# A third product of halves in block form, and the additions of bv moved behind the block sums

## The chip, the cores and the metric

The kernel runs on one core of one Trainium2 chip. A core has TensorE (matrix products, into PSUM), VectorE, ScalarE, GpSimd, and SyncE with the DMA queues. In profile lines they are PE (PEld for weight loads), DVE, ACT, POOL and SP. Each engine works through its own list of instructions in order, and semaphores hold an instruction back until the data it needs, or the buffer it overwrites, is free. The metric is the device time of one execution in microseconds, and less is better.

## The reference

The input `x` has 128 batches of a 128 x 512 matrix (128 nodes, 512 features). All values are float32. Layer 0 normalises each row, takes the positive part, multiplies by the adjacency matrix and adds the largest value per node to `x`. Layer 1 is attention with 8 heads of 64 over the 128 nodes.

```python
# layer 0
h = jnp.maximum(_layernorm(x, axis=-1), 0.0)
A = jnp.einsum('od,bdn->bon', adj, h); C = A + b[None, :, None]
pre = A[:, :, None, :] + (C - A)[:, :, :, None]
x = x + jnp.max(jax.nn.relu(pre), axis=-1)
# layer 1
h = jnp.maximum(_layernorm(x, axis=-1), 0.0)
q = (h @ Wq + bq); k = (h @ Wk + bk); v = (h @ Wv + bv)   # 8 heads of 64
scores = einsum('bihd,bjhd->bhij', q, k) / 8, masked where adj == 0
x = x + einsum('bhij,bjhd->bihd', softmax(scores), v)
```

In layer 0, `A` cancels in `pre`, and what is left per node is the positive part of the largest value of `C`. It adds the same number to all features of a node, so the second normalisation gives the same `h` as the first. That is why the kernel normalises only once.

## The kernel before

The 128 batches go through in 32 groups of four. `x` sits in SBUF in pairs of batches. Each group goes through these steps:

- `norm` and `norm_end`: statistics on VectorE (`bn_stats`, `bn_aggr`, `+eps`), `rstd` and `nmr` on GpSimd, then `h = relu(x*rstd + nmr)` on ScalarE. `norm_end` also calls `add_bv`, a GpSimd addition of bv to `x` for the output.
- `blocks` and `move`: h is transposed in 32 x 32 blocks by VectorE, and 16 DMAs per pair of batches put the blocks into `hT`.
- `adjacency`: one TensorE product, then a maximum on VectorE.
- `Products`: the three projections q, k, v of a group.
- `scores`: q against k, with `exp` on ScalarE; `mask` multiplies by the pattern of the adjacency, on GpSimd.
- `apply`: weights against v, with reciprocal and scaling on VectorE; `residual` adds `x` and writes out.

**The projections.** A projection is a product of a 512 x 512 weight with the group's `hT`. It is cut into quarters, and the four quarters of the result come from seven products of halves, in Winograd's form of Strassen's method, in place of eight. The sums of weight quarters (`s1` to `s4`, `weight_sum`) are made once. The sums of h quarters (`t1` to `t4`, `h_sum` at L340, tile `hs`) are made once per group on VectorE. The products are:

- `p1` = a11·b11
- `p6` = s2·t2
- `p2` = a12·b21
- `p7` = s3·t3
- `p5` = s1·t1
- `p4` = a22·t4
- `p3` = s4·b22

Each is four matmuls of 128 x 128 x 256, written by `mm` (L413 to L425), so eight block products of 128 x 128 x 128. `p4` and `p3` are cut once more by the same method, into seven block products each (`p43a` at L492, `p43b` at L511, matmuls in `block_mm` at L487). For that GpSimd makes block sums of t4 and b22 (`h_blocks` at L347) and, once, block sums of the weights (`weight_blocks` at L361). Parts that several output blocks share go to a scratch bank of PSUM, bank 6, and VectorE adds them on with `more` (L489 to L490). The first and the last group's v uses the plain `p4` and `p3`.

**Order.** The order is written out by hand. Iteration `g` runs `apply(g - 1)`, `scores(g)`, then v of group g and q and k of group g + 1. The 18 entries of `part` (6 for v, 6 for q, 6 for k, numbered 0 to 17 and called steps here) are run in turn, and after each the entries of `todo` for that step. Until the change the sums `t1` to `t4` stand at steps 0, 1, 2, 2 and the block sums at 5 and 6 (for g > 0). `next_norms` places the norms of the batches of group g + 2.

**Buffers.** PSUM has eight banks. v and k use banks 0, 1, 2 for `self.a`, `self.b`, `self.c`, and q uses 3, 4, 5. `hs` is in a pool with two buffers, and `h2` in one with one.

Of the kernel before, what the change touches and what calls it, by code (L numbers as in the profile page):

```python
# [45 lines left out]
F32 = mybir.dt.float32  # L46
# [6 lines left out]
P = 128  # L53
G = 4
H, HD = 8, 64
# [112 lines left out]
def tile_adj_preln_d2(  # L168
# [14 lines left out]
    B, D, N = x.shape  # L183
# [4 lines left out]
    const = ctx.enter_context(tc.tile_pool(name="const", bufs=1))  # L188
# [1 line left out]
    W = {n: const.tile([P, NC, N], F32, name=f"w{n}_sb") for n in "qkv"}  # L190
    WS = {n: const.tile([P, 4, 2, N // 2], F32, name=f"s{n}_sb") for n in "qkv"}

    WB = {n: const.tile([P, 2, 4, P], F32, name=f"ss{n}_sb") for n in "qkv"}
    b0_sb = const.tile([P, 1], F32, name="b0_sb")
    bq_sb = const.tile([P, NC], F32, name="bq_sb")
    bk_sb = const.tile([P, NC], F32, name="bk_sb")
# [10 lines left out]
    def fast(ctx):  # L207
        xpool = ctx.enter_context(tc.tile_pool(name="xpool", bufs=7))
        proj = ctx.enter_context(tc.tile_pool(name="proj", bufs=2))
        one = ctx.enter_context(tc.tile_pool(name="one", bufs=1))  # L210
# [6 lines left out]
        X, HN, TB, HT, HB, H2, QT, KT, C, AMAX, WA, RSTD, NMR, PR = ({} for _ in range(14))  # L217

        def bank(k):

            return ps.tile([P, 512], F32, name=f"bk{k}")
# [63 lines left out]
            nmr = NMR[m] = stat.tile([P, 1], F32, name="nmr")  # L285
            nc.gpsimd.tensor_scalar(nmr, mv[:, 0:1], rstd, -1.0, op0=ALU.mult, op1=ALU.mult)  # L286

        def norm_end(m):
            nc.scalar.activation(HN[m], x_of(m), AF.Relu, scale=RSTD[m], bias=NMR[m])  # L289
            if m >= G:  # L290
                add_bv(m)

        def add_bv(m):
# [52 lines left out]

        def h_blocks(g, k):  # L347

            if k == 0:
                H2[g] = one.tile([P, 2, 4, D], F32, name="h2")  # L350
            b = HB[g]["b22 t4".split()[k]].rearrange("p t c d -> p c t d")
            t = H2[g][:, 1 - k]

            for o, x, y in (
                (t[:, 0:2], b[:, :, 1], b[:, 0]),
                (t[:, 2], b[:, 1, 1], t[:, 0]),
                (t[:, 3], b[:, 1, 0], t[:, 2]),
            ):
                nc.gpsimd.tensor_tensor(o, x, y, op=ALU.subtract)

        def weight_blocks(eng, n):  # L361

            for k in range(2):
                a = WA[n]["a22 s4".split()[k]].rearrange("p c (o f) -> p o c f", o=2)
                s = WB[n][:, k]
                for o, x, op, y in (
                    (s[:, 0], a[:, 1, 0], ALU.add, a[:, 1, 1]),
                    (s[:, 2], s[:, 0], ALU.subtract, a[:, 0, 0]),
                    (s[:, 1], a[:, 0, 0], ALU.subtract, a[:, 1, 0]),
                    (s[:, 3], a[:, 0, 1], ALU.subtract, s[:, 2]),  # L370
                ):
                    eng.tensor_tensor(o, x, y, op=op)
# [19 lines left out]
        class Products:  # L392
# [78 lines left out]
            def block_views(self):  # L471

                self.wa = [
                    WA[self.n][k].rearrange("p c (o f) -> p o c f", o=2) for k in ("a22", "s4")
                ]
                self.hb = [
                    HB[self.g][k].rearrange("p t c d -> p c t d") for k in ("t4", "b22")
                ]
                self.scr = bank(6).rearrange("p (m k d) -> p m k d", m=2, k=2)
                o_t = "(o d) -> p {} o t d" if self.n == "v" else "(t d) -> p {} o t d"  # L480
                r = "t" if self.n == "v" else "o"
                self.ub = self.u.rearrange(f"p k {r} " + o_t.format("k"), d=D)
                self.bk = lambda x: x.rearrange(f"p {r} " + o_t.format(""), d=D)

            def block_mm(self, out, w, h, start=False):
                lhs, rhs = (h, w) if self.n == "v" else (w, h)
                nc.tensor.matmul(out, lhs, rhs, start=start, stop=True, skip_group_check=True)  # L487

            def more(self, to, what):  # L489
                nc.vector.tensor_tensor(to, to, what, op=ALU.add)  # L490

            def p43a(self):  # L492

                self.block_views()
                s, t = WB[self.n], H2[self.g]
                for k in range(2):
                    self.block_mm(
                        self.scr[:, 0, k], self.wa[k][:, 0, 0], self.hb[k][:, 0, 0], start=k == 0
                    )
                for k in range(2):  # L500
                    self.block_mm(self.scr[:, 1, k], s[:, k, 0], t[:, k, 0])
# [8 lines left out]

            def p43b(self):  # L511

                s, t, u, scr = WB[self.n], H2[self.g], self.ub, self.scr
                bc = [self.bk(self.b), self.bk(self.c)]
                for k in range(2):
                    self.block_mm(scr[:, 0, k], s[:, k, 2], t[:, k, 2])
                self.more(u[:, :, 0, 1], scr[:, 0])
                for k in range(2):
                    a, b = self.wa[k], self.hb[k]
                    self.block_mm(bc[k][:, 0, 0], a[:, 0, 1], b[:, 1, 0])  # L520
                    self.block_mm(bc[k][:, 0, 1], s[:, k, 3], b[:, 1, 1])
                    self.block_mm(bc[k][:, 1, 0], a[:, 1, 1], t[:, k, 3])
                for k in range(2):
# [120 lines left out]
        def next_norms(m):  # L644

            return {
                0: [(norm_end, m), (norm_end, m + 1)],
                4: [(blocks, m)], 6: [(blocks, m + 1), (move, m + 1)], 7: [(adjacency, m)],
                8: [(norm, m + 2), (norm_end, m + 2)],
                12: [(norm, m + 3), (norm_end, m + 3), (adjacency, m + 1)],  # L650
                13: [(blocks, m + 2)],
                14: [(blocks, m + 3), (move, m + 3), (adjacency, m + 2)],
            }

        with tc.manual_schedule():
# [31 lines left out]
            k = Products(0, "k")  # L687
# [12 lines left out]
            for g in range(NG):  # L700
                b = g * G
# [108 lines left out]
```

## Time and profile before

| | us |
|---|---|
| median of 10 runs | 1539.22 |
| lowest, highest | 1538.95, 1540.11 |
| profiled execution | 1538.79 |
| its span, first to last instruction | 1537.0 |

The groups of instructions that matter to the steps below, from the page (count, busy time, mean of one):

| line, engine, tiles, shape | count | busy us | mean ns |
|---|---|---|---|
| L490 DVE, u += scratch bank, 128x256 | 552 | 205.5 | 413 |
| L345 DVE, sums of h, 128x512 | 128 | 152.8 | 1194 |
| L469 DVE, sum of `p7`, 128x512 | 95 | 65.3 | 687 |
| L279 DVE, statistics, 128x512 | 128 | 87.5 | 683 |
| L302 DVE, transposition of h, 128x512 | 124 | 83.7 | 693 |
| L295 POOL, bv, 128x512 | 128 | 186.2 | 1465 |
| L582 POOL, mask, 128x512 | 240 | 297.3 | 1271 |
| L359 POOL, block sums of h, 128x256 | 62 | 45.2 | 728 |
| L359 POOL, block sums of h, 128x128 | 124 | 57.8 | 466 |

The page counts busy time per engine over the whole span. A mean can mix two durations: L345 has a median of about 695 ns and a longest of 1766 ns. The trace models the ends of matmuls, so rows of TensorE that follow each other overlap by 0.1 to 0.2 us, and the starts give their spacing. One group takes about 47.4 us: v starts at 803.76 us in the group used below, q at 817.28, k at 829.90.

### The profile page before, as it was taken

What the parts mean: (1) busy time and instruction counts of PE and PEld (TensorE: products, weight loads), DVE (VectorE), ACT (ScalarE), POOL (GpSimd) and SP (SyncE); (2) the same over time, 40 slices, a digit from 0 to 9 for tenths busy, and PEclk for the clock granted to TensorE, in tenths of its full rate; (3) what the DMA queues carried; (4) which work ended last, traced back from release to release, by engine and by line L of the source; (5) the groups of instructions that cost most, each with busy time, mean ns of one, the idle gap of its engine ahead of it and who ended that gap; (6) DMA issues with size and microseconds to landing.
All of it is one profiled execution on the core that took longest, in us unless ns stands there. A gap on an engine that the chain in (4) does not pass through costs nothing. (4 is left out here: it accounts for less than half of the span.)

```text
span 1537.0 us, 33066 instructions
## 1 busy us (share of the span) xinstructions
PE 1506.2 (98%) x12909; PEld 1321.0 (86%) x12909; DVE 1079.0 (70%) x2187; ACT 506.9 (33%) x970; POOL 869.5 (57%) x968
## 2 busy tenths in 40 slices
PE   8999999999999999999999999999999999999997
PEld 6888888888888888888888888888888888888887
DVE  6677677776767767677767777676676767776676
ACT  4333324333233332333332333324333233333332
POOL 5676556556575565655655655656556465565620
PEclk9999999999999999999999999999999999999999
DMA  5222222223222232222322222322223222232211
GB/s 169 60 62 77 63 60 72 65 74 84 42 73 66 72 82 43 76 74 63 79 59 63 74 63 75 74 51 72 65 72 84 42 74 68 70 80 54 52 34 57
DMA packets 307806, 105.32 MB, mean 69 GB/s; under 512 B 273152, under 2 KB 273280, under 8 KB 307648
## 3 DMA queue, kind: packets, MB, share of 16 engines
q1 hardware_dynamic: 307328, 102.84, 26.1%
q8 instruction: 104, 1.70, 0.5%
q14 instruction: 54, 0.44, 0.1%
q0 software_dynamic: 176, 0.27, 0.1%
q10 hardware_dynamic: 144, 0.07, 0.0%
HBM read 37.03 MB, written 33.55 MB: 46 GB/s over the span
## 5 line engine op out<-in xcount | busy, mean ns | idle before, releaser
L630 POOL TENSOR_TENSOR o<-xp,o 128x512 f32<-128x512 f32 x122 | 151.0, 1268 | 312.6 <-DVE o L618 269.3
L582 POOL TENSOR_TENSOR w<-w,live 128x512 f32<-128x512 f32 x240 | 297.3, 1271 | 0.0
L490 DVE TENSOR_TENSOR u<-u,bk 128x256 f32<-128x256 f32 x552 | 205.5, 413 | 120.4 <-PE bk L487 113.3
L578 ACT ACTIVATE w<-bk 128x512 f32<-128x512 f32 x256 | 128.8, 628 | 345.9 <-PE bk L570 345.9
L295 POOL TENSOR_TENSOR xp<-xp,bv_sb 128x512 f32<-128x512 f32 x128 | 186.2, 1465 | 61.3 <-ACT hn L289 60.4
L421 PEld LDWEIGHTS bk<-hs,sk_sb 128*128 128x128 f32 x768 | 143.6, 190 | 44.7 <-issue 29.4
L421 PE MATMUL bk<-hs,sk_sb 128*128 128x256 f32 x768 | 181.3, 379 | 0.0
L421 PE MATMUL bk<-sv_sb,hs 128*128 128x256 f32 x768 | 181.2, 379 | 0.0
L421 PE MATMUL bk<-hs,sq_sb 128*128 128x256 f32 x744 | 175.8, 379 | 0.0
L421 PEld LDWEIGHTS bk<-sv_sb,hs 128*128 128x128 f32 x768 | 143.6, 190 | 31.1 <-issue 14.3
L328 DVE TENSOR_REDUCE amax<-bk 128x1 f32<-128x512 f32 x128 | 88.1, 689 | 105.6 <-PE bk L327 102.7
L421 PEld LDWEIGHTS bk<-hs,sq_sb 128*128 128x128 f32 x744 | 138.9, 190 | 17.6
L284 POOL TENSOR_TENSOR rstd<-ve,mhalf 128x1 f32<-128x1 f32 x128 | 83.5, 653 | 94.2 <-DVE ve L282 93.9
L289 ACT ACTIVATE hn<-xp,nmr,rstd 128x512 f32<-128x512 f32 x124 | 100.7, 813 | 105.0 <-POOL nmr L286 105.0
L469 DVE TENSOR_TENSOR u<-bk,u 128x512 f32<-128x512 f32 x95 | 65.3, 687 | 91.8 <-PE bk L421 89.7
L327 PE MATMUL bk<-hn,adjT 128*128 128x512 f32 x248 | 126.6, 592 | 0.0
L600 PE MATMUL bk<-v,w 128*64 128x65 f32 x4096 | 126.5, 222 | 0.0
L600 PEld LDWEIGHTS bk<-v,w 128*64 128x64 f32 x4096 | 122.1, 137 | 4.1 <-issue 0.3
L421 PE MATMUL bk<-wv_sb,hT 128*128 128x256 f32 x512 | 124.3, 386 | 0.0
L570 PE MATMUL bk<-qT,kT 64*128 64x128 f32 x2048 | 122.9, 275 | 0.0
L421 PE MATMUL bk<-hT,wk_sb 128*128 128x256 f32 x512 | 121.2, 380 | 0.1
L570 PEld LDWEIGHTS bk<-qT,kT 64*128 64x128 f32 x2048 | 116.8, 188 | 2.5 <-issue 0.3
(149 smaller groups left out, 2572.7 us busy)
## 6 DMA issues: line engine op xcount, KB each, us to landing
out_dram<-o SPq DMA_DIRECT2D x128, 256.0 KB, 2.0
xp<-in_x_dram SPq DMA_DIRECT2D x62, 512.0 KB, 3.8
hT<-tb SPq DMA_DIRECT2D x992, 32.0 KB, 1.9
xp<-in_x_dram SPq DMA_DIRECT2D x4, 256.0 KB, 4.2
wq_sb<-in_L_gnn_Wq_dram SPq DMA_DIRECT2D x2, 512.0 KB, 7.6
wk_sb<-in_L_gnn_Wk_dram SPq DMA_DIRECT2D x2, 512.0 KB, 9.7
wv_sb<-in_L_gnn_Wv_dram SPq DMA_DIRECT2D x2, 512.0 KB, 10.2
bv_sb<-in_L_gnn_bv_dram POOLq DMA_DIRECT2D x1, 256.0 KB, 7.6
```

The source lines that it names most:

```text
L284: nc.gpsimd.tensor_tensor(rstd, ve, mhalf, op=ALU.pow)
L289: nc.scalar.activation(HN[m], x_of(m), AF.Relu, scale=RSTD[m], bias=NMR[m])
L295: nc.gpsimd.tensor_tensor(x_m, x_m, bv_sb, op=ALU.add)
L327: nc.tensor.matmul(pa, adjT, HN[m], start=True, stop=True)
L328: nc.vector.reduce_max(AMAX[g][:, i : i + 1], pa, axis=AX.X)
L421: nc.tensor.matmul(bank[:, r, :], lhs, rhs, start=first and r == 0 and c == 0, stop=r == 1 and c == 1, skip_group_check=True,)
L490: nc.vector.tensor_tensor(to, to, what, op=ALU.add)
L570: nc.tensor.matmul(psc[j][:, f, :], KT[g][r, f, i * D : (i + 1) * D], QT[g][r, f, i * D : (i + 1) * D], start=True, stop=True,)
L578: nc.scalar.activation(w[:, j], psc[j], AF.Exp, scale=HD ** -0.5)
L582: eng.tensor_tensor(w[:, j], w[:, j], live_h, op=ALU.mult)
L600: nc.tensor.matmul(pav[r, c : c + HE], w[:, h % 2, h // 2, r], V[:, i, h, :], start=True, stop=True,)
L630: eng.tensor_tensor(y, x_of(b), y, op=ALU.add)
```

## The change

There are four connected edits:

1. `p2` is cut into seven block products too, for q and k of groups 1 to 31 and for v of groups 1 to 30. A third set of block sums is added: `a12` for the weights, `b21` for h. `p2a` computes block products 1 and 5 into a bank that is free (bank 2 for q, bank 5 for v and k), and three block products on top of `p1`'s bank. ScalarE then writes the quarter, and VectorE adds 1 and 5 to it. `p2b` adds block product 6 to what block product 1 left in the bank, `p2c` adds 7, and VectorE adds the result to the quarter each time, with `more2`.
2. `hs` gets a single buffer, and the three sets of block sums a tile each. `t1`, `t2` stand at step 5, `t3`, `t4` at step 6, and the block sums at 5 (b21, b22) and 6 (t4).
3. `add_bv` of the first two batches of a group leaves `norm_end` for step 6, behind the block sums in GpSimd's order. `blocks` of these batches goes from steps 4 and 6 to 1 and 2, `move` from 6 to 5.
4. The last VectorE additions of `p43b` become `p43c`. In v they run at the start of step 6 (behind `t1`, `t2`), ahead of q's `p1` in the program.

In VectorE's list, per product, the additions of 1 and 5 stand before what follows at that step (transposition, statistics or maximum) and before `p7`'s sum; the addition after `p2b` stands directly behind `p7`'s sum. `p2b` waits for the additions of 1 and 5, and `p2c` for the addition after `p2b`.

```diff
-    WB = {n: const.tile([P, 2, 4, P], F32, name=f"ss{n}_sb") for n in "qkv"}
+    WB = {n: const.tile([P, 3, 4, P], F32, name=f"ss{n}_sb") for n in "qkv"}
...
-        def norm_end(m):
+        def norm_end(m, bv=True):
             nc.scalar.activation(HN[m], x_of(m), AF.Relu, scale=RSTD[m], bias=NMR[m])
-            if m >= G:
+            if m >= G and bv:
                 add_bv(m)
...
-            hs = proj.tile([P, 4, 2, 2, D], F32, name="hs")
+            hs = one.tile([P, 4, 2, 2, D], F32, name="hs")
...
-            if k == 0:
-                H2[g] = one.tile([P, 2, 4, D], F32, name="h2")
-            b = HB[g]["b22 t4".split()[k]].rearrange("p t c d -> p c t d")
-            t = H2[g][:, 1 - k]
+            b = HB[g]["t4 b22 b21".split()[k]].rearrange("p t c d -> p c t d")
+            t = H2[g, k] = one.tile([P, 4, D], F32, name=f"h2{k}")
...
-            for k in range(2):
-                a = WA[n]["a22 s4".split()[k]].rearrange("p c (o f) -> p o c f", o=2)
+            for k in range(3):
+                a = WA[n]["a22 s4 a12".split()[k]].rearrange("p c (o f) -> p o c f", o=2)
...
+            def blocks_in(self, bank, k):
+
+                a, b, s, t = self.wa[k], self.hb[k], self.s[:, k], self.t[k]
+                self.block_mm(bank[:, 0, 0], a[:, 0, 1], b[:, 1, 0])
+                self.block_mm(bank[:, 0, 1], s[:, 3], b[:, 1, 1])
+                self.block_mm(bank[:, 1, 0], a[:, 1, 1], t[:, 3])
+
+            def block(self, out, k, m):
+
+                if m == 1:
+                    self.block_mm(out, self.wa[k][:, 0, 0], self.hb[k][:, 0, 0], start=k != 1)
+                else:
+                    e = {5: 0, 6: 2, 7: 1}[m]
+                    self.block_mm(out, self.s[:, k, e], self.t[k][:, e])
...
+            def more2(self, o, t, what):
+
+                d = self.dst(0, 0)
+                if self.n == "v":
+                    d = d.rearrange("p t (o h) d -> p o t h d", o=2)
+                    what = what.rearrange("p (h d) -> p h d", d=HD)
+                else:
+                    d = d.rearrange("p o (t d) -> p o t d", t=2)
+                to = d[:, o, t]
+                if len(to.shape) > len(what.shape):
+                    what = what.unsqueeze(1).to_broadcast(to.shape)
+                self.more(to, what)
+
+            def p2a(self):
+
+                self.block_views()
+                x = bank(2 if self.n == "q" else 5)
+                self.sum2, five = x[:, 0:D], x[:, D : 2 * D]
+                self.block(self.sum2, 2, 1)
+                self.block(five, 2, 5)
+                self.blocks_in(self.bk(self.a), 2)
+                self.biased(self.dst(0, 0), self.a, 0)
+                self.more2(0, 0, self.sum2)
+                self.more2(slice(0, 2), 1, five)
+
+            def p2b(self):
+                self.block(self.sum2, 2, 6)
+                self.more2(0, 1, self.sum2)
+
+            def p2c(self):
+                self.block(self.sum2, 2, 7)
+                self.more2(1, slice(0, 2), self.sum2)
...
-                for k in range(2):
-                    self.block_mm(scr[:, 0, k], s[:, k, 1], t[:, k, 1])
+                for k in range(2):
+                    self.block(self.scr[:, 0, k], k, 7)
+
+            def p43c(self):
                 for i in range(2):
-                    self.more(u[:, :, 1, i], scr[:, 0])
+                    self.more(self.ub[:, :, 1, i], self.scr[:, 0])
                 self.add(self.dst(1, 0), self.b, self.u[:, 0])
                 self.add(self.dst(0, 1), self.c, self.u[:, 1])
...
-                0: [(norm_end, m), (norm_end, m + 1)],
-                4: [(blocks, m)], 6: [(blocks, m + 1), (move, m + 1)], 7: [(adjacency, m)],
+                0: [(norm_end, m, False), (norm_end, m + 1, False)],
+                1: [(blocks, m)], 2: [(blocks, m + 1)],
+                5: [(move, m + 1)], 6: [(add_bv, m), (add_bv, m + 1)], 7: [(adjacency, m)],
...
-                    part += [[p.p1], [p.p6], [p.p2]]
                     if p.n == "v" and g in (0, NG - 1):
-                        part += [[p.p7], [p.p5], [p.p4, p.p3]]
+                        part += [[p.p1], [p.p6], [p.p2], [p.p7], [p.p5], [p.p4, p.p3]]
                     else:
-                        part += [[p.p7, p.p43a], [p.p5], [p.p43b]]
+                        part += [
+                            [p.p1], [p.p6], [p.p2a], [p.p7, p.p2b, p.p43a, p.p2c], [p.p5],
+                            [p.p43b, p.p43c],
+                        ]
+                        if p.n == "v":
+                            late = part[-1].pop()
+                    if p.n == "q" and g > 0:
+                        part[6].insert(0, late)
...
-                    for k, s in enumerate((0, 1, 2, 2) if g > 0 else (3, 3, 4, 5)):
+                    for k, s in enumerate((5, 5, 6, 6)):
                         add(s, h_sum, g + 1, k)
-                    for k, s in enumerate((5, 6)):
+                    for k, s in ((2, 5), (1, 5), (0, 6)):
                         add(s, h_blocks, g + 1, k)
```

More of the change, by code (lines that the diff above doesn't have):

```diff
@@ L473, in block_views @@
                 self.wa = [
-                    WA[self.n][k].rearrange("p c (o f) -> p o c f", o=2) for k in ("a22", "s4")
+                    WA[self.n][k].rearrange("p c (o f) -> p o c f", o=2)
+                    for k in ("a22", "s4", "a12")
                 ]
                 self.hb = [
-                    HB[self.g][k].rearrange("p t c d -> p c t d") for k in ("t4", "b22")
+                    HB[self.g][k].rearrange("p t c d -> p c t d") for k in ("t4", "b22", "b21")
                 ]
-                self.scr = bank(6).rearrange("p (m k d) -> p m k d", m=2, k=2)
+                self.s = WB[self.n]
+                self.t = [H2[self.g, k] for k in range(3)]
                 o_t = "(o d) -> p {} o t d" if self.n == "v" else "(t d) -> p {} o t d"
@@ L489, in more @@
             def more(self, to, what):
                 nc.vector.tensor_tensor(to, to, what, op=ALU.add)
-            def p43a(self):
-                self.block_views()
-                s, t = WB[self.n], H2[self.g]
-                for k in range(2):
[L497 to L501, printed above, removed]
+            def more2(self, o, t, what):
[9 more added lines that the diff above has]
+                self.more(to, what)
@@ L502, in p43a @@
+            def p2c(self):
+                self.block(self.sum2, 2, 7)
+                self.more2(1, slice(0, 2), self.sum2)
+            def p43a(self):
+                self.scr = bank(6).rearrange("p (m k d) -> p m k d", m=2, k=2)
+                for m in (1, 5):
+                    for k in range(2):
+                        self.block(self.scr[:, m // 5, k], k, m)
                 self.more(self.ub[:, :, 0, 0], self.scr[:, 0])
@@ L511, in p43b @@
             def p43b(self):
-                s, t, u, scr = WB[self.n], H2[self.g], self.ub, self.scr
-                bc = [self.bk(self.b), self.bk(self.c)]
                 for k in range(2):
-                    self.block_mm(scr[:, 0, k], s[:, k, 2], t[:, k, 2])
-                self.more(u[:, :, 0, 1], scr[:, 0])
+                    self.block(self.scr[:, 0, k], k, 6)
+                self.more(self.ub[:, :, 0, 1], self.scr[:, 0])
+                for k, x in enumerate((self.b, self.c)):
+                    self.blocks_in(self.bk(x), k)
                 for k in range(2):
[L519 to L523, printed above, removed]
-                    self.block_mm(scr[:, 0, k], s[:, k, 1], t[:, k, 1])
+                    self.block(self.scr[:, 0, k], k, 7)
+            def p43c(self):
                 for i in range(2):
-                    self.more(u[:, :, 1, i], scr[:, 0])
+                    self.more(self.ub[:, :, 1, i], self.scr[:, 0])
                 self.add(self.dst(1, 0), self.b, self.u[:, 0])
```

## The prediction

> **What bounds the kernel now.** I read the page's busy shares first, then the table of waits, then the timeline of each engine over one group (four batches) in the middle of the run.
>
> ```profile
> PE 1506.2 (98%) x12909; PEld 1321.0 (86%) x12909; DVE 1079.0 (70%) x2187; ACT 506.9 (33%) x970; POOL 869.5 (57%) x968
> PEclk9999999999999999999999999999999999999999
> ```
>
> TensorE is busy 98% of the span at full clock, so time is gained only by fewer matmuls or fewer TensorE waits. The table of waits names one recurring wait (total us, times, longest):
>
> ```profile
> PEld bk L487 <- DVE u L490: 27.3, 29, 1.1
> ...
> PE bk L487 <- DVE u L490: 15.7, 29, 0.7
> ```
>
> 29 times means once in each of groups 1 to 29. TensorE's timeline (start, length) shows where: at the start of `p43b` of v.
>
> ```profile
> 811.63 0.38 PE L487 MATMUL bk<-wv_sb,hs 128*128 128x128 f32 x2
> ...
> 812.52 1.89 PE L421 MATMUL bk<-sv_sb,hs 128*128 128x256 f32 x8
> 814.95 0.71 PE L487 MATMUL bk<-ssv_sb,h 128*128 128x128 f32 x4 [0.54 <-DVE u L490]
> 815.50 0.39 PE L487 MATMUL bk<-wv_sb,hs 128*128 128x128 f32 x2
> ```
>
> Starts are the safe reading, since modelled ends overlap. A full product of a half is 1.728 us (772 to 790 us: 775.95 to 777.68, and so on), a block product 0.2225 (815.50, 815.72, 815.94). Unhindered, the block at 815.50 would start at 812.52+1.73+0.445 = 814.69: one stall costs 0.81 us, 0.70 of wait and 0.1 of restart (first pair 0.55 instead of 0.445). VectorE was late because two of its sums of h were slow while GpSimd added bv:
>
> ```profile
> 809.05 0.69 DVE L345 TENSOR_TENSOR hs<-hT,hs 128x512 f32<-128x512 f32 x1
> 809.67 1.76 DVE L345 TENSOR_TENSOR hs<-hT 128x512 f32<-128x512 f32 x1
> 811.35 1.76 DVE L345 TENSOR_TENSOR hs<-hT,hs 128x512 f32<-128x512 f32 x1
> 813.03 0.68 DVE L469 TENSOR_TENSOR u<-bk,u 128x512 f32<-128x512 f32 x1
> 813.81 1.08 DVE L490 TENSOR_TENSOR u<-u,bk 128x256 f32<-128x256 f32 x3
> ```
> ```profile
> 806.97 0.54 POOL L284 TENSOR_TENSOR rstd<-ve,mhalf 128x1 f32<-128x1 f32 x1
> 807.61 0.26 POOL L286 TENSOR_SCALAR nmr<-mv,rstd 128x1 f32<-128x1 f32 x1
> 807.83 1.02 POOL L284 TENSOR_TENSOR rstd<-ve,mhalf 128x1 f32<-128x1 f32 x1
> 808.94 0.27 POOL L286 TENSOR_SCALAR nmr<-mv,rstd 128x1 f32<-128x1 f32 x1
> 809.17 3.39 POOL L295 TENSOR_TENSOR xp<-xp,bv_sb 128x512 f32<-128x512 f32 x2
> ```
>
> Group 30 has no bv left to add. Its sums take 0.68 us, and its `p43b` starts 1.73 us after `p5` (1475.86, 1477.59), without the stall:
>
> ```profile
> 1473.00 0.68 DVE L345 TENSOR_TENSOR hs<-hT 128x512 f32<-128x512 f32 x1
> 1473.60 0.68 DVE L345 TENSOR_TENSOR hs<-hT,hs 128x512 f32<-128x512 f32 x1
> ```
>
> **The Trainium skill.** "SBUF — State Buffer", section "Who interferes with whom": a VectorE instruction with two SBUF inputs contends with a GpSimd one that reads SBUF, and one with at most one SBUF input does not. The trace agrees: sums of h 1.76 against 0.69 us, while L490 (one input in PSUM) stays at 0.35 to 0.41 beside GpSimd. "Perfetto Trace Analysis", section "Tensor Engine Instruction (MATMUL, LD_WEIGHTS)": ends of matmuls are estimated, VectorE, ScalarE and GpSimd are strict FIFO. The first is why I use starts; the second means that in VectorE's queue an addition waits for all ahead of it, as the L469 row above waits for the slow sums.
>
> **Removed: matmuls.** `p2` was 1.728 us; seven blocks are 7 x 0.2225 = 1.558. So 0.170 saved, in 30 products of v (groups 1 to 30), 31 of q, 31 of k: 92 x 0.170 = -15.7 us, all on TensorE.
>
> **Removed: the stall in v.** bv now comes after the block sums. The sums of h stand at steps 5 and 6, since their buffer is single: t1 waits for the fourth block of `p43b`, 1.1 us before v ends on TensorE, and t2 is done 0.3 after v's end, while q's `p6` needs it at 1.73. t3 starts 2.2 after v's end; GpSimd's middle block sums end at 2.04 (as 770.16 to 771.95 after v's end at 769.91 now) and the next wait for t4. So all four cost about 0.69, and nothing in v waits for them: 29 x 0.81 = -23.5 us.
>
> **Added: waits inside each product.** After `p2a`, ScalarE writes the quarter; VectorE adds block 1 (128 columns), then block 5 (256); `p2b` waits for both; `p7`'s sum follows in VectorE's queue, then the addition after `p2b`; `p2c` waits for that. Behind `p2c` TensorE has `p5`: its wait is a pure loss. Prices: TensorE's end to ScalarE or VectorE 0.20 (775.95 to 776.15); ScalarE to VectorE 0.04 (28.23+0.81 to 29.08); VectorE to TensorE 0.06 (814.89 to 814.95); an independent VectorE instruction starts 0.08 before its predecessor's end. No row has a 128-column addition of this kind. From above: L618 128x128, 0.29, with 0.41 for 256 columns. From below: L490's shortest, 0.38 for 256, less 128 columns at 0.96 GHz ("VectorE: DVE Perf Modes", section "The TRN2 errata — SBUF-src ops pay a fixed extra latency per instruction": one column per cycle for fp32; the trace's 0.29 and 0.41 give 0.12 us for 128 columns, about the same), so 0.25. L490's median is 0.41, its shortest 0.38, so I work the chains through at the lower pair, then at the upper, and take the middle. `p2c` is ready 1.73+0.22+0.89 = 2.84 us after `p2a` ends (k: 0.86 later, an adjacency matmul lies between). Clock 0 is that end:
>
> - **q** (VectorE: adds, then the statistics of the next batch, then `p7`'s sum). ScalarE 0.20 to 1.04, second add 1.08 to 1.46, statistics from 1.38 for 1.15 (775.04 to 776.19 below), `p7`'s sum 2.45 to 3.14, add 3.06 to 3.31, release 3.37: 0.53 late, with restart 0.63. Now the statistics lie in VectorE's idle 1.76 us:
>
> ```profile
> 775.04 0.68 DVE L279 BATCH_NORM_STATS2 st<-xp 128x6 f32<-128x512 f32 x1
> 775.82 0.18 DVE L280 BATCH_NORM_AGGREGATE mv<-st 128x2 f32<-128x6 f32 x1
> 776.04 0.15 DVE L282 TENSOR_SCALAR ve<-mv 128x1 f32<-128x1 f32 x1
> 777.95 0.69 DVE L469 TENSOR_TENSOR u<-bk,u 128x512 f32<-128x512 f32 x1 [1.76 <-PE bk L421]
> ```
> - **k**: GpSimd's five masks (6.20 us) end 17.3 us into q instead of 15.6, pushed back by bv and the block sums, and k starts at 13.1. So the last batch's rstd starts 4.2 us into k, its norm on ScalarE ends at 5.9, and the quarter, ready at 5.63, is written 0.23 late. Second add 1.31 to 1.69, transposition to 2.31, maximum to 2.92, sum to 3.53, add to 3.70, release 3.76 against 3.70: 0.06, with restart 0.16.
> - **v**: clock from v's start (803.76). `p2a` ends at 5.52 (808.17, where `p2` starts now, and five blocks). ScalarE does the second norm first: GpSimd's second rstd falls from 1.02 to 0.55 without sums of h beside it, so that norm ends at 5.82 (now 810.05, 6.29). The first moved transposition (0.70) is done by 6.0, before the quarter; the second stands behind the adds. Copy to 6.40, adds 6.44 to 6.69 and 6.61 to 6.99 (`p2b` ready at 7.25, no wait), transposition to 7.61, sum to 8.22, add to 8.39, release 8.45 against 8.36: 0.09, with restart 0.19.
>
> Sum at the lower pair: 30 x 0.19 + 31 x 0.63 + 31 x 0.16 = +30.2 us. At 0.29 and 0.41 the three are 0.29, 0.70, 0.23: +37.5. The middle is +33.9. As the bound from below, no wait in k and v and 0.3 in q: +9.3.
>
> **Other edits.** Twelve instead of eight block sums of weights and three more GpSimd block sums per group (0.73+2x0.48 = 1.7 us) lie in GpSimd's idle time (4.97 and 9.29 us per group); without that cover, 1.7 x 30 = 51 us. The two moved additions of bv (1.27 each) end 7.7 us into q, before GpSimd's next rstd, which has its statistics at 8.0. `late` moves v's last additions behind t1 and t2, but before bank 2 is needed (2.3 against 4.3 us into q). SP's queue has the same DMAs; the 16 moves are issued a step earlier, behind the same end of v. Edges: group 0's t1 waits for v's plain last product (+0.5); 1.8 us of weight sums ahead of group 1's residuals (+0.6); in group 30 masks stand where k had little (+0.6). Together +1.7, bounds 0 and 4.
>
> Sum on the profiled execution: 1538.79 (span 1537.0 plus 1.8 around it) - 15.7 - 23.5 + 33.9 + 1.7 = 1535.2; the runs' median is 0.4 higher: **1535.6**. Its own range, from the lower pair and the edges' bounds, is 1530 to 1538.
>
> **Rivals.**
> - *The added waits are nearly all hidden*: +9.3 instead of +33.9 gives 1511. For: VectorE now has 1 to 1.8 us idle before these sums. Against: the statistics alone fill most of it in q.
> - *Given back entirely*: the upper prices, 1535.6 + 3.6 = 1539.2, and 1538 to 1543 if one more of these chains is 0.1 us later than counted (30 x 0.1 = 3). For: the only 128-column row of this kind is L618, and L490's median is at the upper price.
> - *ScalarE late in v (slower)*: if GpSimd's second rstd stays at 1.0 us, the copy starts 0.47 later; `p2b` is then 0.28 late with restart 0.38 and `p2c` again 0.2: 0.6 to 0.76 per v instead of 0.24, +11 to +16: 1547 to 1551, or 1555 with the upper prices; 1550 in the middle. It decides from 0.12 us of lateness on (30 x 0.12 = 3.6, all of the gain). For: ScalarE's copy now follows that norm by only 0.05 us. Against: nothing with two SBUF inputs is left there.
>
> **Numbers.** What can be told from no change is 0.2%, 3.1 us. Forecast 0.42 (0.34 faster, 0.08 same), hidden 0.23 (faster), given back 0.18 (0.10 same, 0.08 slower), ScalarE late 0.17 (slower): faster 0.57, same 0.18, slower 0.25. The range 1507 to 1549 leaves out half of the last rival and the tail of the first, about 0.17.
>
> **What would show it.** `p43b` of v loses its wait for L490; `p2c` waits for VectorE, about 0.5 us in q and 0.1 in k and v; sums of h at 0.69; the second rstd at 0.55. Wrong if sums of h stay at 1.76, if `p2b` waits in v, or if `p2c` in q shows no wait.

## The result and the profile after

| | before | after |
|---|---|---|
| median of the runs, us | 1539.24 (28 runs) | 1532.15 (8 runs, 1530.6 to 1533.59) |
| ratio | | 0.9954, 95% interval 0.9945 to 0.9963 |
| profiled execution, us | 1538.79 | 1532.03 |
| its span, us | 1537.0 | 1530.3 |

The kernel is 0.46% faster: 7.1 us, where 3.6 were forecast. The page of the changed kernel (busy us, share, instructions; then the granted clock in 40 slices):

```profile
PE 1501.4 (98%) x13461; PEld 1334.6 (87%) x13461; DVE 1119.2 (73%) x2559; ACT 500.7 (33%) x970; POOL 887.6 (58%) x1069
PEclk9999999999999999999999999999999999999999
```

TensorE still fills the span, at the same clock. More and smaller matmuls do less work; VectorE has 372 instructions more. The table of waits (engine and line, what it waited for; total us, times, longest) no longer has the 29 stalls behind L490 (L505 is now the line of these additions). In their place stands another wait of once per group:

```profile
PEld bk L487 <- DVE qT L505: 16.1, 30, 0.6
...
PE bk L487 <- DVE qT L505: 10.4, 30, 0.4
```

It is q's `p2c`. TensorE's timeline of one group in the middle (start, length), v first and then q. The last row of a fence can be cut by the window shown and then counts only the matmuls inside it (x3 of 8 here):

```profile
809.67 0.98 PE L487 MATMUL bk<-ssv_sb,h 128*128 128x128 f32 x6
810.49 1.89 PE L419 MATMUL bk<-sv_sb,hs 128*128 128x256 f32 x8
812.22 0.61 PE L487 MATMUL bk<-ssv_sb,h 128*128 128x128 f32 x4
...
822.27 0.61 PE L487 MATMUL bk<-h,ssq_sb 128*128 128x128 f32 x4
823.23 0.49 PE L487 MATMUL bk<-h,ssq_sb 128*128 128x128 f32 x2 [0.34 <-DVE qT L505]
823.55 0.81 PE L419 MATMUL bk<-hs,sq_sb 128*128 128x256 f32 x3
```

In v, `p43b` follows `p5` after 1.73 us (810.49, 812.22): its stall is gone. But the three blocks that end with `p2c` take 0.82 us (809.67 to 810.49) where three take 0.667: 0.15 is lost, and the trace names no wait for it. In q they take 1.28 (822.27 to 823.55): 0.61 lost. In k, read in the same way, 0.12. Together 0.88 us a group.

VectorE's timeline in the same q shows what `p2c` waits for:

```profile
820.59 0.79 DVE L505 TENSOR_TENSOR qT<-qT,bk 128x128 f32<-128x128 f32 x2 [0.93 <-ACT qT L434]
821.29 0.69 DVE L279 BATCH_NORM_STATS2 st<-xp 128x6 f32<-128x512 f32 x1
...
822.23 0.15 DVE L282 TENSOR_SCALAR ve<-mv 128x1 f32<-128x1 f32 x1
822.30 0.68 DVE L467 TENSOR_TENSOR u<-bk,u 128x512 f32<-128x512 f32 x1
822.90 0.28 DVE L505 TENSOR_TENSOR qT<-qT,bk 128x128 f32<-128x128 f32 x1
```

The short addition at 822.90 releases TensorE at 823.23. It stood in the queue behind the sum of `p7` (0.68), and that behind the statistics, although `p7`'s matmuls had ended by 821.61. The sums of h, on VectorE at v's end, are the second thing to read:

```profile
813.37 0.69 DVE L345 TENSOR_TENSOR hs<-hT 128x512 f32<-128x512 f32 x1
814.09 0.69 DVE L345 TENSOR_TENSOR hs<-hT,hs 128x512 f32<-128x512 f32 x1
...
816.69 0.68 DVE L345 TENSOR_TENSOR hs<-hT 128x512 f32<-128x512 f32 x1
817.29 0.68 DVE L345 TENSOR_TENSOR hs<-hT,hs 128x512 f32<-128x512 f32 x1
```

All four take 0.68 to 0.69. In the whole run only three sums of the first group, which run beside GpSimd's sums of weights in both kernels, still take 1.64 to 1.75; before, 61 did. The spans by parts, from the starts of `scores` (groups 2 to 29 as a mean):

| part | before | after | difference |
|---|---|---|---|
| start of the span to `scores(0)` | 43.42 | 44.64 | +1.22 |
| group 0 | 46.03 | 47.22 | +1.19 |
| group 1 | 47.37 | 48.67 | +1.30 |
| groups 2 to 29, each | 47.38 | 46.98 | -0.40, 28 times -11.19 |
| group 30 | 44.58 | 47.03 | +2.45 |
| `scores(31)` to the end | 29.11 | 27.39 | -1.72 |
| span | 1537.0 | 1530.3 | -6.7 |

So 11.2 us were gained in the repeated groups, and 6.2 lost in the start and three edge groups. Of the last row nothing lies in the work: ScalarE's copy of the flag comes 22.56 us after `scores(31)` before and 22.57 after; only what follows the last instructions is shorter, and it differs from kernel to kernel (this row lies between 27.4 and 29.4 us in the kernels below). The first row is no effect of the change either. Up to `scores(0)` TensorE, VectorE and ScalarE have the same instructions in both kernels, and GpSimd the same ones up to the norms that k waits for; but GpSimd's first sum of weights, which waits for the weights to arrive, starts 1.2 us later (before, then after):

```profile
17.07 1.56 POOL L384 TENSOR_TENSOR sv_sb<-wv_sb 128x512 f32<-128x512 f32 x1 [6.97 <-DMA wv_sb<-in_L_gnn_Wv_dram]
...
18.27 1.58 POOL L382 TENSOR_TENSOR sv_sb<-wv_sb 128x512 f32<-128x512 f32 x1 [7.52 <-DMA wv_sb<-in_L_gnn_Wv_dram]
```

In the two kernels below that begin exactly like before (e1, e7) it starts at 16.68 and 17.95, and in those that begin like after it lies between 16.8 and 18.2. Two of the edge losses stand in TensorE's timeline of after, one in group 1's v (`p2b`) and one in group 30's q:

```profile
104.36 0.49 PE L487 MATMUL bk<-ssv_sb,h 128*128 128x128 f32 x2 [1.11 <-DVE v L505]
...
1479.25 1.99 PE L419 MATMUL bk<-hs,sq_sb 128*128 128x256 f32 x8 [2.01 <-DVE u L458]
```

and the second has its reason on VectorE:

```profile
1476.34 0.65 DVE L680 TENSOR_SCALAR tb<-RS 128x960 f32<-128x960 f32 x1
1477.02 1.56 DVE L681 SCALAR_TENSOR_TENSOR tb<-RS,tb 128x960 f32<-128x960 f32 x1
...
1478.51 0.68 DVE L458 TENSOR_TENSOR u<-bk,p1a 128x512 f32<-128x512 f32 x1
```

In group 30 `count` (L680, L681) is at step 6, where the sums t3 and t4 now stand too. It runs behind them, and `p6`'s sum (L458) behind it; q's `p7`, which adds to the bank that this sum reads, waits 2.0 us.

### The profile page after: what moved, and what is told of

Its sections match the earlier page's. It is cut to its first block, busy times and chain, and to the rows that moved or that the text cites. A ratio compares the mean times of both kernels' runs of the same rounds, so it can differ in the third digit from the quotient of the medians.

```text
span 1530.3 us, 34887 instructions
## 1 busy us (share of the span) xinstructions
PE 1501.4 (98%) x13461; PEld 1334.6 (87%) x13461; DVE 1119.2 (73%) x2559; ACT 500.7 (33%) x970; POOL 887.6 (58%) x1069
## 5 line engine op out<-in xcount | busy, mean ns | idle before, releaser
L505 DVE TENSOR_TENSOR u<-u,bk 128x256 f32<-128x256 f32 x552 | 206.0, 415 | 88.4 <-PE bk L487 88.3
L295 POOL TENSOR_TENSOR xp<-xp,bv_sb 128x512 f32<-128x512 f32 x128 | 161.2, 1271 | 59.5 <-ACT hn L289 59.5
L419 PEld LDWEIGHTS bk<-hs,sk_sb 128*128 128x128 f32 x768 | 143.5, 190 | 44.6 <-issue 29.4
L357 POOL TENSOR_TENSOR h<-hT 128x256 f32<-128x256 f32 x62 | 45.9, 740 | 188.0 <-PE bk L487 186.8
L487 PE MATMUL bk<-h,ssq_sb 128*128 128x128 f32 x558 | 95.6, 280 | 10.4 <-DVE qT L505 10.4
L659 DVE TENSOR_TENSOR o<-bk,RS 128x448 f32<-128x448 f32 (+1 forms) x161 | 93.7, 582 | 7.2
L487 PEld LDWEIGHTS bk<-h,ssq_sb 128*128 128x128 f32 x558 | 81.6, 191 | 19.6 <-DVE qT L505 16.1
```

The source lines that it names most:

```text
L295: nc.gpsimd.tensor_tensor(x_m, x_m, bv_sb, op=ALU.add)
L419: nc.tensor.matmul(bank[:, r, :], lhs, rhs, start=first and r == 0 and c == 0, stop=r == 1 and c == 1, skip_group_check=True,)
L659: nc.vector.tensor_tensor(oo, po[:, :, 0:HD], rs.unsqueeze(2).to_broadcast([P, rs.shape[1], HD]), op=ALU.mult,)
```

## The experiments

Each ratio is to the kernel before, timed beside the run. A "period" below is the time from one `scores` to the next in the repeated groups (the median): 47.37 us before, 46.96 after. All medians and intervals:

| run | starts from | median us | ratio to before, 95% interval | period us |
|---|---|---|---|---|
| e1: bv moved, alone | before | 1521.41 | 0.9881 (0.9865 to 0.9898) | 46.75 |
| e2: statistics a step earlier | after | 1525.05 | 0.9907 (0.9890 to 0.9923) | 46.74 |
| e3: plain `p2` | after | 1517.96 | 0.9862 (0.9846 to 0.9879) | 46.565 |
| e4: bv put back | after | 1532.69 | 0.9954 (0.9937 to 0.9970) | 46.96 |
| e5: e2 and e4 | after | 1517.07 | 0.9855 (0.9839 to 0.9872) | 46.48 |
| e6: transpositions behind `p7` | e5 | 1515.71 | 0.9844 (0.9827 to 0.9860) | 46.465 |
| e7: bv and one transposition | before | 1516.42 | 0.9851 (0.9835 to 0.9868) | 46.565 |
| e8: edges | e6 | 1515.69 | 0.9843 (0.9827 to 0.9860) | 46.465 |
| e10: `p7`'s sum behind the addition | after | 1510.48 | 0.9808 (0.9792 to 0.9824) | 46.21 |
| e9: the same, with e8 | e8 | 1502.92 | 0.9763 (0.9747 to 0.9779) | 46.083 |

### e1: is the stall in v due to bv?

```diff
...
-                0: [(norm_end, m), (norm_end, m + 1)],
-                4: [(blocks, m)], 6: [(blocks, m + 1), (move, m + 1)], 7: [(adjacency, m)],
+                0: [(norm_end, m, False), (norm_end, m + 1, False)],
+                4: [(blocks, m)],
+                6: [(blocks, m + 1), (move, m + 1), (add_bv, m), (add_bv, m + 1)], 7: [(adjacency, m)],
```

> The kernel before with nothing changed but the place of bv: the additions for the first two batches of a group stand behind the block sums, at step 6. Theory (the wait of p43b in v comes from two sums of h slowed by GpSimd's bv): the wait goes in all 29 groups, 29 x 0.81 = 23.5 us, so about 1516 us, and all sums of h take about 0.69 us. Rival (VectorE is late in v whatever bv does): the wait stays, 1537 to 1541 us.

1521.41 us. The wait at the start of `p43b` is gone and all sums of h after the first group take about 0.69, so the cause of that wait is shown: this part of the change alone takes 18 us off the kernel before, 11 more than the whole change. But the period fell by 0.62, not 0.81. The rest is at the end of v's `p43b`. TensorE in this run, then VectorE:

```profile
806.87 0.39 PE L487 MATMUL bk<-sv_sb,h 128*128 128x128 f32 x2
807.18 0.71 PE L487 MATMUL bk<-ssv_sb,h 128*128 128x128 f32 x4
807.73 1.89 PE L421 MATMUL bk<-hT,wq_sb 128*128 128x256 f32 x8
```
```profile
806.12 0.70 DVE L302 STREAM_TRANSPOSE tb<-hn 128x512 f32<-128x512 f32 x1
806.74 0.38 DVE L490 TENSOR_TENSOR u<-u,bk 128x256 f32<-128x256 f32 x1
```

The last blocks start 0.31 after 806.87 instead of 0.2225, and behind a wait a pair costs 0.55 instead of 0.445 (807.18 to 807.73). They wait for the addition at 806.74, and that for a transposition of h ahead of it.

### e7: the transposition

```diff
-                4: [(blocks, m)],
+                1: [(blocks, m)],
```

> The kernel before with bv moved behind the block sums, and the first transposition of h moved from step 4 of v to step 1. With bv alone 0.62 us a group went instead of 0.81. Theory: the missing 0.19 is the transposition standing ahead of the block sum in p43b on VectorE; then this run is 5 to 6 us below that of bv alone, 1516 us, and the second wait of p43b in v is gone. Rival: the 0.19 is the cost of the wait through the half bank itself; then 1521, no change.

1516.42 us and a period of 46.565, which is 0.805 below before, once the transposition that e1 left at step 4 stands at step 1. The stall counted as 0.81 is worth that in full, but only with both moves; the change contains both.

### e4: does the change need the move of bv?

```diff
-                0: [(norm_end, m, False), (norm_end, m + 1, False)],
+                0: [(norm_end, m), (norm_end, m + 1)],
...
-                5: [(move, m + 1)], 6: [(add_bv, m), (add_bv, m + 1)], 7: [(adjacency, m)],
+                5: [(move, m + 1)], 7: [(adjacency, m)],
```

> The changed kernel with bv of the first two batches back in norm_end at step 0, all else as changed. Theory (in the changed order the sums of h stand at steps 5 and 6, away from bv, so the move of bv is not needed any more): no wait comes back in v, sums of h stay at 0.69 us; GpSimd's masks end earlier, ScalarE is no longer late in k, and the time is 1527 to 1532 us. Rival (the move of bv is what removed the wait): 10 to 24 us more, 1542 to 1556 us.

1532.69 us: as with the move. In the new order the sums of h stand at v's end and no longer beside bv, so either move alone removes the overlap. The expectation of k was wrong, as GpSimd's timeline of this run shows:

```profile
806.66 2.51 POOL L295 TENSOR_TENSOR xp<-xp,bv_sb 128x512 f32<-128x512 f32 x2
...
822.32 0.55 POOL L284 TENSOR_TENSOR rstd<-ve,mhalf 128x1 f32<-128x1 f32 x1 [2.60 <-DVE ve L282]
```

bv runs from 806.66 to 809.17 and is out of the way, but after the block sums GpSimd waits 2.60 us for the statistics on VectorE (`ve`). They, not bv and the block sums, set when GpSimd gets to its masks, and so when the last norm of k is done.

### e3: what is the cut of `p2` worth?

```diff
-                            [p.p1], [p.p6], [p.p2a], [p.p7, p.p2b, p.p43a, p.p2c], [p.p5],
+                            [p.p1], [p.p6], [p.block_views, p.p2], [p.p7, p.p43a], [p.p5],
```

> The changed kernel with p2 as four plain matmuls again in q, k and v, and without p2a, p2b, p2c; order of all else, buffers and the third set of block sums on GpSimd stay. Theory (the blocks save 0.51 us of matmuls per group and cost 0.88 us of waits): per group 0.37 us less, with the edges 12 to 15 us less than the changed kernel: 1517 to 1520 us. Rival (the blocks are the gain, and the order only makes room for them): 15.7 us more, 1548 us.

1517.96 us, within the range expected: with `p2` plain and all the rest of the change in place the kernel is 14 us faster. TensorE's table of waits has no entry of 30 times for another engine, and the period of 46.565 is that of e7. So the cut of `p2` loses 0.40 us a group net in this order.

### e2 and e5: the statistics ahead of `p7`'s sum

e2 moves the statistics of batch m + 2 from q's `p2a` to the step before. e5 does that and puts bv back as in e4.

```diff
-                5: [(move, m + 1)], 6: [(add_bv, m), (add_bv, m + 1)], 7: [(adjacency, m)],
-                8: [(norm, m + 2), (norm_end, m + 2)],
+                5: [(move, m + 1)], 6: [(add_bv, m), (add_bv, m + 1)], 7: [(adjacency, m), (norm, m + 2)],
+                8: [(norm_end, m + 2)],
```

> The changed kernel with the statistics of the third batch (norm of m + 2) one step earlier, at step 7, so that they stand ahead of the additions of p2a on VectorE and not between them and p7's sum. Theory (the wait of p2c in q is the statistics in front of p7's sum): p2c of q is late by at most 0.1 us instead of 0.5, and about 31 x 0.5 = 15 us go: 1517 us. Rival (p2c waits for p2b's own addition and its latency): the wait stays above 0.3 us, 1528 to 1533 us.

1525.05 us, 7 better than after and 8 short of the expectation. TensorE's timeline, first the last three blocks of q's step, then k's:

```profile
817.75 0.96 PE L487 MATMUL bk<-h,ssq_sb 128*128 128x128 f32 x6
...
831.19 1.22 PE L487 MATMUL bk<-h,ssk_sb 128*128 128x128 f32 x6
832.25 1.03 PE L419 MATMUL bk<-hs,sk_sb 128*128 128x256 f32 x4
```

In q the three blocks now take 0.80 (the next product is at 818.55), a loss of 0.13 instead of 0.61. In k they take 1.06, a loss of 0.39 instead of 0.12. GpSimd shows why:

```profile
815.28 2.50 POOL L295 TENSOR_TENSOR xp<-xp,bv_sb 128x512 f32<-128x512 f32 x2
817.74 0.54 POOL L284 TENSOR_TENSOR rstd<-ve,mhalf 128x1 f32<-128x1 f32 x1
```

The statistics are now there at 816.1, but rstd waits behind bv until 817.74. Counted from q's start, the masks end only 0.2 earlier than in after, while k starts 0.48 earlier, so ScalarE's norm and, behind it, the quarter of k are late. With the first limit gone, bv is the next one.

> The changed kernel with the statistics of the batch m + 2 one step earlier AND bv of the first two batches back behind their normalization. If the wait of q's last block comes from the statistics on VectorE, and the wait of k that grew in their earlier run comes from GpSimd's two additions of bv ahead of rstd, both are small here: 0.13 in q, 0.1 or less in k, about 0.4 to 0.5 us a group less than the changed kernel, 1517 us (1514 to 1520). Rival: k's lateness comes from k starting earlier while the masks end when they did, whatever stands ahead of rstd; then k keeps 0.3 to 0.4 and the run is at 1525.

1517.07 us, as the theory had it: the two moves that gave 7 us and nothing apart give 15 together. Three losses of 0.13 to 0.14 are left, one in each product.

### e6: are the transpositions what is left?

```diff
-                1: [(blocks, m)], 2: [(blocks, m + 1)],
+                1: [(blocks, m)], 3: [(blocks, m + 1)],
...
-                14: [(blocks, m + 3), (move, m + 3), (adjacency, m + 2)],
+                14: [(adjacency, m + 2)], 15: [(blocks, m + 3), (move, m + 3)],
```

> The kernel of e5 with two transpositions of h on VectorE moved from ahead of the sum of p7 and the block sum of p2b to behind them (v: step 2 to 3, k: step 14 to 15). Theory: they are what makes p2c wait 0.15 in v and about 0.1 in k, so about 0.25 us a group goes, 7 to 8 us below e5. Rival: in v and k the wait is the bare latency of a block, its addition and the next block through one half bank, and the order on VectorE doesn't matter: within 2 us of e5.

1515.71 us: the rival was right. VectorE now idles before the sum of `p7` in v, and the three blocks take 0.80 us all the same. VectorE, then TensorE, in this run:

```profile
800.10 0.69 DVE L467 TENSOR_TENSOR u<-bk,u 128x512 f32<-128x512 f32 x1 [0.50 <-PE bk L419]
800.71 0.28 DVE L505 TENSOR_TENSOR v<-v,bk 128x128 f32<-128x128 f32 x1
```
```profile
799.90 0.38 PE L487 MATMUL bk<-ssv_sb,h 128*128 128x128 f32 x2
...
800.57 0.96 PE L487 MATMUL bk<-ssv_sb,h 128*128 128x128 f32 x6
801.37 0.81 PE L419 MATMUL bk<-sv_sb,hs 128*128 128x256 f32 x3
```

`p7`'s matmuls end at 799.90. The sum starts 0.20 later and holds VectorE for 0.61 before the addition (0.28) can start; with 0.06 to TensorE that is 1.15 us. TensorE has five blocks for that time, 1.11 us, and then pays the restart of about 0.1. The chain is too long by itself; nothing foreign has to stand in it.

### e10: one change of order

`p7` is divided into its matmuls and its sum on VectorE, and the sum is issued after `p2b` with its addition.

```diff
...
                 self.mm(self.b, "s3", "t3")
+
+            def p7_sum(self):
                 self.u3 = tmp.tile([P, 2, HT2], F32, name="u3", bufs=1)
...
-                            [p.p1], [p.p6], [p.p2a], [p.p7, p.p2b, p.p43a, p.p2c], [p.p5],
+                            [p.p1], [p.p6], [p.p2a], [p.p7, p.p2b, p.p7_sum, p.p43a, p.p2c], [p.p5],
```

> The changed kernel with one change of order alone: VectorE's sum of p7 is issued after the addition of p2b's block instead of before it (p7's matmuls stay where they are). Theory after e6: p2c waits for the chain p7's last matmul, 0.20, p7's sum 0.61 to 0.69, addition 0.28, 0.06, which is longer than the five blocks between; with the sum behind the addition the chain is out of the way in all three products, in q too, since 0.6 of the sum comes off the statistics' lateness. The three waits of p2c (0.15, 0.61, 0.12) are then nearly gone: 0.75 to 0.88 us a group, 1505 to 1510 us. Rival: p5's addition or p43's additions, which come after the sum, become late and the gain is given back there: 1518 or more.

1510.48 us, at the upper end of the expectation: 22 us less than the changed kernel, from the order of two VectorE instructions. TensorE and VectorE in q, where L489 are the blocks, L507 the additions and L469 the sum of `p7` in this kernel:

```profile
811.73 0.85 PE L489 MATMUL bk<-h,ssq_sb 128*128 128x128 f32 x6
812.41 0.81 PE L419 MATMUL bk<-hs,sq_sb 128*128 128x256 f32 x3
```
```profile
811.68 0.15 DVE L282 TENSOR_SCALAR ve<-mv 128x1 f32<-128x1 f32 x1
811.75 0.28 DVE L507 TENSOR_TENSOR qT<-qT,bk 128x128 f32<-128x128 f32 x1
811.95 0.68 DVE L469 TENSOR_TENSOR u<-bk,u 128x512 f32<-128x512 f32 x1
```

The statistics are still where they were, the three blocks take 0.68, and nothing behind the sum became late in the repeated groups. In k 0.12 stays (825.06 to 825.85), where ScalarE writes the quarter late and a transposition and a maximum still stand ahead of the addition on VectorE.

Two edge groups of this execution took longer than in after: group 1 50.02 us and group 30 47.85. TensorE waits 1.9 and 2.0 us there, and shortly behind these waits the trace has a granted clock of 0.5 for 3.41 us, in which the rows of blocks start 0.213 apart instead of 0.112. In after the wait of 2.01 in group 30 is followed by the full clock, so these runs show no rule for it.

### e8 and e9: the edges, and all of it together

e8 is e6 with three things moved: `count` in group 30 to step 11, that group's masks to GpSimd, and one mask of each group from step 10 to 13. e9 is e8 with the split of e10 and the masks at their old steps; in group 1 alone the statistics are issued ahead of the residuals.

```diff
-                        add(6, count, 0, b)
-                    eng = nc.gpsimd if m < B else nc.vector
-                    at = (8, 9, 9, 10, 10, 13, 14, 15) if m < B else (4, 8, 8, 12, 12, 13, 14, 14)
+                        add(11, count, 0, b)
+                    eng = nc.gpsimd
+                    at = (8, 9, 9, 10, 13, 13, 14, 15)
```

> The kernel of e6 with three things at its edges and in k: the first count of the row sums (2.2 us of VectorE) from step 6 to step 11 of the last but one group, the masks of that group on GpSimd instead of VectorE, and one mask of each group from step 10 to step 13, ahead of which GpSimd then reaches the rstd of the batch m + 3. Expected: the 2.0 us wait of q's p7 and the 0.5 us wait of k in group 30 go, and k's hn is no longer late: 2.5 to 6 us below e6. Rival: VectorE's count is late at another place, or the mask that is moved makes the weights of the next apply late: no gain or a loss.

1515.69 us, no gain. By parts, group 30 took 45.07 us instead of 47.04 in e6, as meant, but group 1 took 48.41 instead of 47.18. There GpSimd has four additions of bv, 12 sums of weight blocks and four residuals ahead of the rstd that group 1's v needs, and the moved mask (1.27) pushes all of them back: counted from the start of group 1, this rstd starts 1.23 later than in e6. The wait in group 1's v is 1.81 us in e8. In group 30 a part of `count` comes back: k's `p7` waits 0.9 for the sum of `p6`.

```diff
+                    if g == 1:
+                        norm(m)
+                        norm(m + 1)
                     if g > 0:
                         for i in range(G):
                             residual(b - G + i, nc.gpsimd)
-                    if m < B:
+                    if m < B and g != 1:
                         norm(m)
                         norm(m + 1)
```

> The kernel of e8 with the sum of p7 behind the addition of p2b's block, the five masks back at their first places, and in group 1 alone the statistics of the next two batches issued ahead of the residuals on GpSimd. The three waits of 0.13 to 0.14 that stay in e6 and e8 in each product go: 30 x 0.40 = 12 us; group 1's v no longer waits for its norms behind the residuals: 1 to 1.9 us. 1499 to 1503 us. Rival: as for the run before, the additions behind the sum are late in their turn: 1510 or more.

1502.92 us, within the range expected. Group 1 takes 46.09 us, group 30 44.79, and the period is 46.083. The page of e9, and the table of waits for TensorE's matmuls:

```profile
PE 1484.0 (99%) x13461; PEld 1327.8 (88%) x13461; DVE 1118.1 (74%) x2551; ACT 504.1 (34%) x970; POOL 899.9 (60%) x1077
```
```profile
PE bk L260 <- POOL ident masks.py:199: 4.8, 1, 4.8
PE bk L825 <- DVE live L683: 2.2, 1, 2.2
PE bk L321 <- ACT o L289: 1.9, 1, 1.9
PE bk L419 <- DVE u L458: 1.0, 1, 1.0
```

Each comes once in the run; the rest of the list is shorter than these, and none of 30 times is left. e9 beats before by 2.4% and after by 1.9%, and keeps `p2` in blocks. Its period is 0.48 below that of e7, which has `p2` plain and the same steady groups without a wait: the cut is worth 0.16 for each product, if nothing waits.

## Why the prediction was right, and where not

The direction and the main mechanism held: TensorE gains two things in each group and gives part of it back as waits of `p2c`. By its own steps, in us of the profiled execution:

| step | predicted | measured | from |
|---|---|---|---|
| matmuls | 92 x 0.170 = -15.7 | 92 x 0.161 = -14.8 | e9 against e7 |
| stall in v | 29 x 0.81 = -23.5 | 29 x 0.805 = -23.3 | e7 against before |
| waits of `p2c` | +33.9 | 30 x 0.15 + 31 x 0.61 + 31 x 0.12 = +27.1 | after, v, q and k |
| edges: groups 0, 1, 30 | +1.7 | about +4.5 | table of parts |
| up to `scores(0)` | 0 | +1.2 | table of parts |
| behind the last instructions | 0 | -1.7 | table of parts |
| sum | -3.6 | -7.0; the execution fell by 6.8 | |

In the steady groups the three measured terms make -0.48 - 0.805 + 0.88 = -0.405 us, which is the -0.40 seen. For the edges, groups 0, 1 and 30 lost 4.94 together; the same terms applied to the products and the stall in them account for +0.4 of that, so 4.5 is left.

**The waits** were the step of the sum that was sized wrong. The prediction worked the chains through with two pairs of durations and took the middle of the sums. The lower pair gave 0.19, 0.63 and 0.16; the trace has 0.15, 0.61 and 0.12. The lone addition of 128 columns took 0.27 to 0.28, between the two prices of 0.25 and 0.29. The upper chains gave 0.29, 0.70 and 0.23, and the middle carried half of that excess into the sum: 3.7 of the 6.8 us by which it is too high. The other 3.1 are the 0.02 to 0.04 by which even the lower chains are too long. (The prediction also read the additions of L490 as 0.35 to 0.41; single rows of before take 0.38 to 0.42. The chains don't use the 0.35.) The order of the three, and that q is the worst because of the statistics, were right, and e2, where q loses 0.13 with the statistics a step earlier, shows that they cost the other 0.48.

**The stall** had its main cause named: sums of h at 1.76 us beside GpSimd's bv. But the prediction put all 0.81 on them. With bv alone out of the way 0.62 go (e1), because a second wait then comes up at the end of `p43b`, behind a transposition; it takes the move of that as well to gain the other 0.19 (e7). The change moves the transposition too, and the prediction did not count this in `p43b`, so that the term came out at its full size is partly luck. Group 30, which it took as its evidence, has neither bv nor a transposition and could not tell the two apart. The Trainium skill, "SBUF — State Buffer", section "Who interferes with whom", which the prediction used for this, agrees: with the sums elsewhere, bv at its old place costs nothing (e4), and the sums take 0.69. What the prediction did not say is that in the new order the move of the sums alone is enough to keep them from bv.

**The edges** were sized too small, and one was missed. Group 1 was named (weight sums ahead of its residuals), at 0.6; it lost 1.7 against a steady group (+1.30 where the others have -0.40). Group 30 was to lose 0.6 by its masks: they cost a wait of 0.5 in k, but the larger loss of 2.0 is `count`, which the prediction had not looked at. The rule it states, that in VectorE's queue an addition waits for all ahead of it, would have found it: the diff leaves `count` at step 6 and moves two sums there. Group 0 (+1.19) has the forecast wait for the sums of h: `p6` of q starts late and costs 0.71 by the starts, where 0.5 was forecast; the rest is `p2c` as in the other groups.

The two main errors pull against each other: 6.8 us of waits too many, 2.8 of edges too few. The start and the end, where the work is the same, add +1.2 and -1.7. So the forecast came closer to the result than its steps did, and that is partly luck.

**In k** the prediction had the quarter 0.23 late, because bv and the block sums push GpSimd's masks back. It is 0.21 late, but for another reason: e4 takes bv away and GpSimd waits for the statistics instead. Both have to go (e5) before the quarter is on time. Even then k still loses 0.13, since the chain through `p7`'s sum is as long; so in after the late quarter was not the only limit of k.

**The rivals.** ScalarE is not late in v: the second rstd takes 0.55 us, and `p2b` doesn't wait there in the steady groups; only in group 1 it does, for 1.11. "Given back entirely" fell with the upper prices. "The waits are hidden" (1511) did not happen in this kernel; it is what e10 makes of it, 1510.48, by putting the addition ahead of the sum. The prediction listed that sum in each chain, at 0.61 to 0.69 us, and took its place in the queue as given.

## What to carry to other kernels

A product that is cut into blocks saves TensorE's time only if the sums between the blocks keep up. Where one engine serves both a short addition that TensorE waits for and a longer one that nobody needs yet, the short one goes first: here that order was worth 22 us, more than three times the whole change. When a change has several parts, price each alone: two moves of order gave 23 us (e7), the cut took 14 back beside them (e3), and the sum looked like a small success. A shift of work has to be followed into the first and the last groups as well, where other instructions stand at the same steps.

## What the runs showed that was not expected

- Two moves can each gain little alone and much together. The statistics a step earlier gave 7 us, bv back gave none, both gave 15 (e2, e4, e5): GpSimd's rstd needs both its input and its turn, and the later of the two counts.
- A loss of about 0.14 us in a product may not appear as a wait: the rows of v and k in after carry no bracket, and only the starts (0.79 to 0.82 us for three blocks in place of 0.667) show it. Between e8 and e9 this was 0.38 us a period in three products, 11 us in all.
- The cut of a plain product into seven blocks saved 0.16 us by the period and not the 0.170 forecast. The starts of all matmuls of one repeated group show both prices off by a little: e7 has 24 rows of plain products more than e9, 5.17 us or 1.724 for each product (read as 1.728), and e9 has 42 rows of blocks more, 4.69 us or 0.2232 for each block (read as 0.2225). The difference is 0.48 a group, as the periods have it.
